# Four graph layers on one core: the opening's beta product in halves, scalings between relus, and a step order of its own for the second group

## The chip, the core and the metric

The kernel runs on one core of a Trainium2 chip. The metric is the device time of one execution in microseconds (us). Five engines work beside each other, each through its own list of instructions in order: the tensor engine (PE, for matmuls; its weight loads are counted apart as PEld), the vector engine (DVE), the scalar engine (ACT), GpSimd (POOL) and SyncE (SP). SP does nothing here but start DMA transfers, and POOL hardly more. An engine that waits for something holds back all that stands behind it in its list. Matmul results go to PSUM, which the kernel splits into two pools of four buffers.

## The reference

128 graphs of 64 nodes, with 512 features for each node, go through four layers, all in fp32. Each layer adds its result to x and normalizes the rows:

```python
# layer 0: hypergraph convolutions with H = (adj != 0), w = adj's first row
#   conv(x, W, b) = D^-1 H B^-1 H^T (x W^T) + b
h = relu(conv(x, W1, b1))                 # 512 -> 1024
h = layer_norm(h, gamma, beta)
x = norm(x + conv(h, W2, b2) + x)         # 1024 -> 512
# layer 1: scores from y = x w, s = y a
A = exp(leaky(tanh((s_i + s_j) / 8) * 8)) * adj
A = A / rowsum(A) * rowsum(adj)
x = norm(x + A x w)
# layer 2: three graph convolutions, relu after the first two
x = norm(x + adj (relu(adj (relu(adj (x gW1) + gb1) gW2) + gb2) gW3) + gb3)
# layer 3: eight heads of attention
p = 0.33 softmax(mask(q k^T / 8)) + 0.33 adj + 0.33 exp(-adj)
x = norm(x + (p v) W_out + b_out)
```

## The kernel before

**Tiles and groups.** Two graphs make one tile of 128 rows (a "pair" in the code), and four tiles make one group of 512 rows. There are 16 groups. A product with a graph's matrix consists of small matmuls of 64x64: `graph_T` (L435 to 453) does it and turns the result for the next product. These are the records named gt_l (layers 0 to 2) and gt_l0h (the 1024 hidden features of layer 0); a call for two tiles is 64 records.

**Products with weights.** From the second group on, every product of a 512x512 block is done in seven smaller products instead of eight (`multiply`, L503). Four sums of the left matrix (`sums`, L471, named s_...) and four differences of the weight (t1 to t4) stand in for blocks. Their order is B11, T1, T2, B21, T3, B22, T4 (L37). After B11, T1 and T2 the PSUM buffer is copied or added to a bias (`snap`; names u_...), and after B21, T3, B22 and T4 DVE or ACT adds the parts into the destination (L531 to 542). Since B11, T2, T3 and T4 go through one buffer (names a_...), each of them waits until the one before it has been read. The other two buffers are named b_... and c_.... One of the seven products is 8 matmuls of 256 columns.

**The weights.** A `Stream` brings weights in the order of their use through a ring of 20 tiles (`pump`, L340), each tile one DMA on SP. For the first use of a weight (q = 0) its four blocks come, DVE makes the four differences (`make`, L256; four subtractions), and POOL's queue writes them to DRAM (L277), from where later groups load them. Before, all weights that are loaded by then are made when the running product reaches its fourth part, B21 (L364), and a first use gives all its 8 ring tiles back after its last part. W2 is special: it has to be scaled by gamma, 16 times `act.mul` (L298, names w2s), and beta times W2 is needed as a row, bw_bc: 32 matmuls into bwps and an ACT copy (`beta_times`, L303).

**The first group** (`first_group`) can't wait for differences and uses plain products of 32 matmuls a tile (`rows_of`, names pp). `hidden(p, n)` is one tile's half of layer 0's first product with the relu; then come the statistics, the roots (`root`, on ACT), the reciprocal and the normalization of h (names rs_h, hb). `wa` builds, in two visits, the row w a for layer 1: a diagonal dg on DVE, one matmul wa_ps, a copy.

**The order.** Two strings at the end of the kernel (L1179 to 1188) write the order by hand. `start` is the opening, and each instruction made in it stays at its place on its engine (`in_turn`, and the wrapper at L132, which is the line that the profile gives for nearly everything up to about 130 us). Then come the steps of `order`: a. is the first half (layers 0 and 1) of group `step`, b. the second half (layers 2 and 3) of the group before, t. the tail (v, softmax, W_out) of the one before that. Each word runs a generator to its next `yield`; `stops` of a product says where it may yield. `rows` and `prep` build the matrices of the next but one group. Outside the opening a scheduler may move instructions by priority; `behind(key)` holds one back until the last addition of the named product has been issued. In step 1 there is no tail.

Of the kernel before, what the change touches and what calls it, by code (L numbers as in the profile page):

```python
# [14 lines left out]
P = 128  # L15
# [7 lines left out]
Q = 256  # L23
# [18 lines left out]
def kernel(  # L42
# [182 lines left out]
    class Weight:  # L225
# [62 lines left out]

        def scale(self):

            quads = []
            for u, raw in enumerate(self.raw):
                s = big.tile([P, 4, 2, Q], FP, name=f"{self.name}s_{u}", tag="big")
                b = {}
                for n, (k, m) in enumerate(((0, 0), (0, 1), (1, 1), (1, 0))):
                    for c in range(2):
                        f = (u * 2 + k) * 2 + c
                        act.mul(s[:, n, c], raw[:, n, c], ga_col[:, f : f + 1])  # L298
                    b[k, m] = s[:, n]
                quads.append(b)  # L300
            return quads

        def beta_times(self):  # L303

            bb = sp.tile([P, DH // P, P], FP, name="bb", tag="s")
            nc.gpsimd.tensor_copy(bb, be_col.unsqueeze(2).to_broadcast([P, DH // P, P]))
            ps = ps_gt.tile([P, 2, Q], FP, name="bwps", tag="gt")
            for n in range(2):
                for c in range(DH // P):
                    u, k, kc = c // 4, c // 2 % 2, c % 2  # L310
                    ten.matmul(
                        ps[:, n, :], bb[:, c, :], self.raw[u][:, ((0, 1), (3, 2))[k][n], kc, :],
                        start=(c == 0 and n == 0), stop=(c == DH // P - 1), skip_group_check=True,
                    )
            act.copy(bw_bc, ps.rearrange("p n f -> p (n f)"))

    w_1 = [Weight(W1T, n * D, f"w1{'ab'[n]}") for n in range(2)]
    w_2 = Weight(W2T, 0, "w2", halves=2, scaled=True)
# [7 lines left out]
    class Stream:  # L326


        def __init__(self, uses):
            self.todo = []  # L330
            for wt, q in uses:
                if q == 0:
                    self.todo.append((wt, q, None, 8))
                else:
                    self.todo += [(wt, q, what, wt.halves) for what in ORDER]
            self.here = {}
            self.held = 0
            self.to_make = []

        def pump(self):  # L340
            while self.todo and self.held + self.todo[0][3] <= RING:
                wt, q, what, n = self.todo.pop(0)
                self.held += n
                if q > 0:
                    self.here[wt, q, what] = [wt.load(q, what, u) for u in range(wt.halves)]
                elif wt in by_pairs:
                    by_pairs[wt] = None if wt.scaled else wt.load_quads()
                else:
                    self.to_make.append((wt, wt.load_quads()))

        def keep(self, wt):

# [8 lines left out]
        def take(self, wt, q, what):  # L361
            self.pump()

            if what == ORDER[3] or (q == 0 and (wt, q) not in self.here):  # L364
                for made, quads in self.to_make:
                    self.here[made, 0] = made.make(quads)
                self.to_make = []
            if q > 0:
                return self.here.pop((wt, q, what))
            return self.here[wt, q][what]  # L370

        def done(self, wt, q, what):

            if q > 0:
                self.held -= wt.halves
            elif what == ORDER[-1]:
                self.held -= 8
            self.pump()

    def load_wa():  # L380
# [122 lines left out]
    def multiply(lefts, wt_q, dst, key, flipped=False, res=None, stops=(3,)):  # L503


        acc = [ps_acc.tile([P, 2, Q], FP, name=f"{n}_{key}", tag="acc") for n in "ab"]

        def snap(ps, m, n, what):
            t = work.tile([P, 2, Q], FP, name=f"{what}_{key}", tag="w")
            if res is None:  # L510
                act.copy(t, ps)
            else:
                vec.tensor_add(t, ps, res(m, n))  # L513
            return t

        pa, pc = acc
        product(pa, lefts, wt_q, B11, True, False, flipped)
        s1 = snap(pa, 0, 0, "u1")
        if 1 in stops:
            yield  # L520
        product(pc, lefts, wt_q, T1, True, False, flipped)
        s5 = snap(pc, 1, 1, "u5")
        if 2 in stops:
            yield
        product(pa, lefts, wt_q, T2, False, False, flipped)
        s2 = snap(pa, 0, 1, "u2")
        if 3 in stops:
            yield
        pb = ps_acc.tile([P, 2, Q], FP, name=f"c_{key}", tag="acc")
        product(pb, lefts, wt_q, B21, True, True, flipped)  # L530
        vec.tensor_add(dst(0, 0), pb, s1)  # L531
        product(pa, lefts, wt_q, T3, False, False, flipped)
        vec.tensor_add(dst(1, 1), pa, s5)  # L533
        if 5 in stops:
            yield
        product(pc, lefts, wt_q, B22, False, True, flipped)
        last_add[key] = vec.tensor_add(dst(0, 1), pc, s2).ins  # L537
        product(pa, lefts, wt_q, T4, False, True, flipped)
        if res is None:
            act.copy(dst(1, 0), pa)  # L540
        else:
            vec.tensor_add(dst(1, 0), pa, res(1, 0))
# [112 lines left out]
    def first_half(g):  # L655
# [9 lines left out]
        for n in range(2):  # L665
            for i, _ in enumerate(multiply(
                [left], (w_1[n], q),
                lambda m, k: h[m][:, :, n * D + k * Q : n * D + (k + 1) * Q],
                f"l0w1{n}_{q}",
                res=lambda m, k: row2(b1_bc, n * D + k * Q),  # L670
                stops=(2, 3) if q == 1 and n == 0 else (3,),
            )):
                yield f"w1{'ab'[n]}{i + 1}"
            yield "w1" + "ab"[n]
# [77 lines left out]
        yield "c3"  # L752
        with behind(f"wo_{q - 2}"):
            left.sums()

        y = big.tile([P, G, D], FP, name=f"y_{q}", tag="big")
        for _ in multiply([left], (w_l1, q), nat(y), f"l1w_{q}", stops=(5,)):
# [21 lines left out]
    def first_group(g):  # L779
# [55 lines left out]
        for m in range(2):  # L835
            mv = small.tile([P, 2, 2], FP, name=f"mvh_0_{m}", tag="mvh")
            for p in range(2):
                hidden(2 * m + p, 1)
                if p > 0:
                    h_stats(2 * m, 1)  # L840
            h_stats(2 * m + 1, 1)
            for p in range(2):
                vec.bn_aggr(mv[:, p, :], sth[:, 2 * m + p].rearrange("p c s -> p (c s)"))
            rs = root(mv, f"h_0_{m}")
            vec.reciprocal(rs, rs)
            for p in range(2):
                normed(h[m][:, p, :], mv, rs, p)
        stream.used(w_1[1])
        yield "w1b"
        lefts = [Left(f"l0h{u}_0") for u in range(2)]  # L850
        for duo in range(2):
            for u in range(2):
                graph_T(
                    lambda p: h[p // 2][:, p % 2, u * D : (u + 1) * D], g["sm"], lefts[u].t, duo, f"l0h{u}_0"
                )
        yield "c2"
        hts = [left.t for left in lefts]
        s4 = small.tile([P, G], FP, name="s4_0", tag="s4")
        e = grp.tile([P, G, C], FP, name="e_0", tag="e", bufs=1)
# [92 lines left out]
        yield "c31"  # L952
        out_of_l1(2)
        out_of_l1(3)
        normed_l1(1)
        stream.used(w_l1)
        yield "l12"

    def second_half(g):
        q, xg = g["q"], g["x"]  # L960
# [62 lines left out]
                vec.tensor_add(xr, ps[p], xr)  # L1023
        yield "agg"

        with behind(f"wo_{q - 1}") if q < NGRP - 1 else nullcontext():
            layer_norm(xg, f"l2_{q}")
        left = Left(f"xT_{q}")

# [124 lines left out]
    def attend(g, duo, pts, v, left):  # L1154
# [22 lines left out]


    start = """  # L1179
        a0.c1 keep0 rest a0.w1a keep1 a0.w1b scale rows0 wa bw a0.c2 doubled0 constant0 rows1 a0.w20 keep2 wa prep1 a0.w21 a0.w22  # L1180
        a0.ss0 a1.c1 a0.w23 a0.den0 doubled1 a0.w24 a0.c30 a1.w1a1 a0.l10 a0.ss1 a0.l11 a0.den1 a1.w1a2 a0.c31 constant1 a1.w1a a0.l12
        a1.resid a1.w1b1 b0.gt a1.w1b keep3
    """.split()
    order = """
        t.v1 a.c1 t.v b.gt t.soft a.w1a1 a.w1a t.soft2 a.resid b.l2a1 b.l2a a.w1b1 t.ptp a.w1b t.pv a.lnh t.osum
        b.l2b1 a.c2a b.l2b a.c2b b.gb3 load a.w21 b.gh a.w2 rows b.l2c1 b.l2c2 a.ss b.l2c t.o1 a.den t.o2 a.c3 b.agg t.o
        a.p1 b.xT a.p2 b.q1 b.q t.ln3 b.k1 prep b.k b.dots
    """.split()
    lag = {"a": 0, "b": 1, "t": 2}
    todo = []  # L1190
# [7 lines left out]
            todo.append((what, 0, None))  # L1198
    n_start = len(todo)
    for step in range(1, NGRP + 2):  # L1200
        for what in order:
            who, dot, name = what.partition(".")
            key = (who, step - lag[who], name) if dot else (what, step + 1, None)
            if 0 <= key[1] < NGRP and key not in todo:
                todo.append(key)
# [17 lines left out]
    with in_turn(SP):  # L1223
        load_adn(first)
        w_2.load_raw()
    for n, (who, q, name) in enumerate(todo):
        opening[0] = n < n_start
        if who == "load":
# [2 lines left out]
        elif who == "rows":  # L1231
            if q > 0:
                preps[q] = prepare(groups[q])
            with behind(f"l0w2_{q - 1}") if q > 1 else nullcontext():
                next(preps[q])
        elif who == "prep":
            next(preps[q])
# [14 lines left out]
        elif who == "rest":  # L1252
            with in_turn(SP, POOL):
# [7 lines left out]
                gb2_col = load_col(gb2, KD, "gb2_col")  # L1261
                gb3_bc = load_row(gb3, D, "gb3_bc")
                bo_bc = load_row(bout, D, "bo_bc")
        elif who == "scale":
            by_pairs[w_2] = w_2.scale()
        elif who == "bw":
            w_2.beta_times()
        else:
            side = "a" if who == "a" else "b"
            if (side, q) not in gens:  # L1270
# [58 lines left out]
```

## Time and profile before

| | |
|---|---|
| median of 3 runs | 2818.47 us (2814.20 to 2824.47) |
| profiled execution | 2818.55 us |
| its span | 2816.8 us |
| PE busy | 2772.3 us |
| DVE busy | 2003.0 us |
| ACT busy | 819.1 us |
| POOL busy | 38.9 us |
| HBM traffic over the span | 143 GB/s |

The profile is one execution; its times count from the start of the span. Busy times of engines overlap. A row of the list of waits gives the engine and the operation that waited, the engine and the operation that released it, then the sum of the waiting time, the number of waits, and their mean. A row of the timeline gives the start, the length, the engine, the line, the operation with output<-input, and in brackets the idle time before it with what ended it; "issue" stands for a wait that the profile can't put down to another engine. The clock of PE is a share of the full clock, averaged over a stretch. A steady step, from the second on, takes 171.8 us; the opening and step 1 reach to about 390 us.

### The profile page before, as it was taken

What the parts mean: (1) busy time and instruction counts of PE and PEld (TensorE: products, weight loads), DVE (VectorE), ACT (ScalarE), POOL (GpSimd) and SP (SyncE); (2) the same over time, 40 slices, a digit from 0 to 9 for tenths busy, and PEclk for the clock granted to TensorE, in tenths of its full rate; (3) what the DMA queues carried; (4) which work ended last, traced back from release to release, by engine and by line L of the source; (5) the groups of instructions that cost most, each with busy time, mean ns of one, the idle gap of its engine ahead of it and who ended that gap; (6) DMA issues with size and microseconds to landing.
All of it is one profiled execution on the core that took longest, in us unless ns stands there. A gap on an engine that the chain in (4) does not pass through costs nothing.

```text
span 2816.8 us, 67748 instructions
## 1 busy us (share of the span) xinstructions
PE 2772.3 (98%) x28862; PEld 2365.4 (84%) x28862; DVE 2003.0 (71%) x3861; ACT 819.1 (29%) x1467; POOL 38.9 (1%) x72
## 2 busy tenths in 40 slices
PE   8999999999999999999999999999999999999998
PEld 7888888888888888888888888888888888888877
DVE  5677677676876767767677676767767677676756
ACT  3223323223232322323223223232323323232222
POOL 2010000000000000000000000000000000000000
PEclk9999999999999999999999999999999999999999
DMA  7354445454544545445454454545545454454441
GB/s 248 109 183 132 129 145 162 125 165 129 153 147 134 162 130 166 129 137 162 128 165 129 140 162 134 157 126 146 157 133 161 132 153 139 131 163 131 147 119 63
DMA packets 309661, 405.94 MB, mean 144 GB/s; under 512 B 57425, under 2 KB 184945, under 8 KB 309361
## 3 DMA queue, kind: packets, MB, share of 16 engines
q1 hardware_dynamic: 304384, 385.84, 46.3%
q0 software_dynamic: 4976, 15.76, 1.5%
q8 instruction: 229, 3.75, 0.6%
q14 instruction: 72, 0.58, 0.1%
HBM read 370.57 MB, written 30.93 MB: 143 GB/s over the span
## 4 chain that ended last, share of the span: by engine, by line
PE 85%; DVE 9%; issue 4%; ACT 1%; DMA 1%; POOL 0%; SPq 0%; DVEq 0%; POOLq 0%
PE a_l0w L496 13%; PE b_l0w L496 7%; PE a_l2b L496 4%; PE a_v L496 4%; PE a_k L496 4%; PE a_q L496 4%; PE c_l0w L496 4%; PE a_l2a L496 4%; PE a_l1w L496 4%; PE gt_l L445 3%; PE a_wo L496 3%; PE gt_l0h L445 2%; PE a_l2c L496 2%; PE b_l2b L496 2%; PE b_v L496 2%
## 5 line engine op out<-in xcount | busy, mean ns | idle before, releaser
L496 PE MATMUL a_l0w<-w2w,aT_l0h 128*128 128x256 f32 x720 | 164.3, 381 | 0.0
L427 DVE BATCH_NORM_STATS2 st_l<-x 128x6 f32<-128x512 f32 x248 | 160.3, 675 | 0.1
L496 PEld LDWEIGHTS a_l0w<-w2w,aT_l0h 128*128 128x128 f32 x720 | 135.6, 190 | 18.8
L681 ACT ACTIVATE h<-h 128x1024 f32<-128x1024 f32 x58 | 61.4, 1059 | 216.4 <-DVE h L537 194.9
L431 DVE TENSOR_SCALAR x<-x,mv_l,rs_l 128x512 f32<-128x512 f32 x248 | 120.1, 545 | 1.8
L453 ACT COPY aT_l<-gt_l 128x512 f32<-128x512 f32 x176 | 90.5, 601 | 72.8 <-PE gt_l L445 72.8
L496 PE MATMUL b_l0w<-w2w,s_l0h 128*128 128x256 f32 x480 | 108.5, 379 | 0.0
L496 PEld LDWEIGHTS b_l0w<-w2w,s_l0h 128*128 128x128 f32 x480 | 90.1, 190 | 13.5
L1002 ACT ACTIVATE aT_h<-gth,gb_col 128x256 f32<-128x256 f32 x128 | 48.5, 490 | 158.9 <-PE gth L994 158.9
L418 ACT ACTIVATE rs_l<-mv_l,eps_t 128x4 f32<-128x4 f32 (+1 forms) x63 | 18.9, 300 | 257.0 <-DVE mv_l L428 255.7
L496 PE MATMUL a_l2b<-gwbw,aT_h 128*128 128x256 f32 x360 | 86.9, 384 | 4.7 <-ACT aT_oT L1174 4.7
L496 PE MATMUL a_l2a<-aT_l,gwaw 128*128 128x256 f32 x360 | 86.6, 383 | 1.0 <-ACT aT_l L453 1.0
L496 PE MATMUL a_q<-aT_xT,wqw 128*128 128x256 f32 x360 | 86.6, 383 | 0.3 <-ACT aT_xT L1041 0.3
L496 PE MATMUL a_v<-wvw,aT_xT 128*128 128x256 f32 x360 | 86.7, 384 | 0.0
L496 PE MATMUL a_l2c<-gwcw,aT_h 128*128 128x256 f32 x360 | 85.3, 380 | 0.7 <-DVE g L533 0.7
L496 PE MATMUL a_wo<-wow,aT_oT 128*128 128x256 f32 x360 | 85.8, 381 | 0.1
L496 PE MATMUL a_l1w<-ww,aT_l 128*128 128x256 f32 x360 | 85.1, 379 | 0.0
L496 PE MATMUL a_k<-aT_xT,wkw 128*128 128x256 f32 x360 | 85.0, 379 | 0.0
L496 PE MATMUL a_l0w<-w1aw,aT_l 128*128 128x256 f32 x336 | 82.3, 388 | 0.0
L496 PE MATMUL a_l0w<-w1bw,aT_l 128*128 128x256 f32 x336 | 81.7, 379 | 0.0
L513 DVE TENSOR_TENSOR u_l0w<-a_l0w,b_bc 128x512 f32<-128x512 f32 x56 | 38.5, 688 | 59.8 <-PE a_l0w L496 59.8
L496 PEld LDWEIGHTS a_l2b<-gwbw,aT_h 128*128 128x128 f32 x360 | 67.1, 190 | 15.2 <-ACT aT_oT L1174 6.6
(503 smaller groups left out, 6474.0 us busy)
## 6 DMA issues: line engine op xcount, KB each, us to landing
w2w<-w2k SPq DMA_DIRECT2D x210, 256.0 KB, 2.7
x<-in_x_dram SPq DMA_DIRECT2D x15, 1024.0 KB, 6.2
w1aw<-w1ak SPq DMA_DIRECT2D x60, 256.0 KB, 2.7
w1bw<-w1bk SPq DMA_DIRECT2D x60, 256.0 KB, 2.7
ww<-wk SPq DMA_DIRECT2D x60, 256.0 KB, 2.7
gwaw<-gwak SPq DMA_DIRECT2D x60, 256.0 KB, 3.5
gwbw<-gwbk SPq DMA_DIRECT2D x60, 256.0 KB, 2.7
gwcw<-gwck SPq DMA_DIRECT2D x60, 256.0 KB, 2.7
```

The costliest lines, as they stand in the source:

```text
L418: act.activation(rs[:, at], mv[:, at, 1], AF.Sqrt, bias=eps_t)
L427: vec.bn_stats(st, xg[:, p, :])
L431: vec.tensor_scalar(xg[:, p, :], xg[:, p, :], mv[:, p, 0:1], rs[:, p : p + 1], ALU.subtract, ALU.mult)
L445: ten.matmul(ps[g][f * C : (f + 1) * C, c, p, :], src(2 * duo + p)[rows, c0 : c0 + C], mat[rows, 2 * duo + p, :], start=True, stop=True,)
L453: act.copy(o[:, :, :, g, :], ps[g])
L496: ten.matmul(acc[:, blk, :], lhsT, rhs, start=(first and blk == 0 and i == 0), stop=(last and i == n_k - 1), skip_group_check=True,)
L513: vec.tensor_add(t, ps, res(m, n))
L681: act.activation(hn, hn, AF.Relu)
L1002: act.activation(o[:, :, h, :], ps[h][:, c].rearrange("p (d a) i -> p d (a i)", d=2), AF.Relu, bias=gb2_col[:, k : k + 1],)
```

## The change

The change rearranges the opening and step 1. Matmuls, elementwise operations and transfers stay the same in kind and number.

1. `scale` becomes a generator with four parts: two blocks at a time (four `act.mul`) are done after each of the four `hidden(p, 1)` of the first group. Before, all sixteen followed the normalization of h.
2. `beta_times` takes its PSUM buffer from the pool of the weight products, `ps_acc`, and not from `ps_gt`. It yields between its halves: 16 matmuls stand ahead of each half of gt_l0h (`c20`, `c21`), and the copy follows the second half.
3. `Stream` makes a weight's differences at the B21 of the product just before that weight's first use, not of any weight that has come. In step 1, `sumsq` and `sumsk` make those of w_q and w_k earlier than that, at places in the order. A first use gives back its ring tiles part by part: two after B11, one after each other part.
4. The start order: `keep3` (the differences of layer 1's w) goes ahead of a1.resid, `a0.l12` ahead of a1.w1b1, and the last normalization of layer 1 for the first group becomes a part of its own, `l13`, behind a1.w1b1. The second stop of a1.w1a is after B21 instead of T2, and a1.w1b gets a stop after T1.
5. Step 1 has an order of its own, `step_1`: the third group's matrices (`rows`) stand behind b.k1 and are held until q's last addition; the layer norm of layer 2 for the first group is held until the sums of layer 1 for the second.

```diff
         def scale(self):
-            quads = []
+            self.quads = []
...
                         act.mul(s[:, n, c], raw[:, n, c], ga_col[:, f : f + 1])
                     b[k, m] = s[:, n]
-                quads.append(b)
-            return quads
+                    if n == 3:
+                        self.quads.append(b)
+                    if n % 2:
+                        yield
         def beta_times(self):
...
-            ps = ps_gt.tile([P, 2, Q], FP, name="bwps", tag="gt")
+            ps = ps_acc.tile([P, 2, Q], FP, name="bwps", tag="acc")
...
+                if n == 0:
+                    yield
             act.copy(bw_bc, ps.rearrange("p n f -> p (n f)"))
+            yield
...
-                    self.to_make.append((wt, wt.load_quads()))
+                    self.to_make[wt] = wt.load_quads()
+
+        def make(self, wt, q):
+            if q == 0 and wt in self.to_make:
+                with in_turn(DVE):
+                    self.here[wt, 0] = wt.make(self.to_make.pop(wt))
...
-            if what == ORDER[3] or (q == 0 and (wt, q) not in self.here):
-                for made, quads in self.to_make:
-                    self.here[made, 0] = made.make(quads)
-                self.to_make = []
+            at = self.uses.index((wt, q))
+            if what == ORDER[3] and at + 1 < len(self.uses):
+                self.make(*self.uses[at + 1])
+            if q == 0:
+                self.make(wt, q)
...
-            elif what == ORDER[-1]:
-                self.held -= 8
+            else:
+                self.held -= 2 if what == ORDER[0] else 1
...
         vec.tensor_add(dst(0, 0), pb, s1)
+        if 4 in stops:
+            yield
...
-                stops=(2, 3) if q == 1 and n == 0 else (3,),
+                stops=((2, 4), (2, 3))[n] if q == 1 else (3,),
...
+        last_add[f"l1s_{q}"] = next(
+            i for i in reversed(nc.cur_bb.bb.instructions) if i.engine == DVE
+        )
...
                 hidden(2 * m + p, 1)
+                next(scaling)
...
-        yield "c2"
+            yield f"c2{duo}"
...
-        normed_l1(1)
         stream.used(w_l1)
         yield "l12"
+        normed_l1(1)
+        yield "l13"
...
-        with behind(f"wo_{q - 1}") if q < NGRP - 1 else nullcontext():
+        with behind(f"wo_{q - 1}" if q > 0 else "l1s_1") if q < NGRP - 1 else nullcontext():
             layer_norm(xg, f"l2_{q}")
...
     start = """
-        a0.c1 keep0 rest a0.w1a keep1 a0.w1b scale rows0 wa bw a0.c2 doubled0 constant0 rows1 a0.w20 keep2 wa prep1 a0.w21 a0.w22
-        a0.ss0 a1.c1 a0.w23 a0.den0 doubled1 a0.w24 a0.c30 a1.w1a1 a0.l10 a0.ss1 a0.l11 a0.den1 a1.w1a2 a0.c31 constant1 a1.w1a a0.l12
-        a1.resid a1.w1b1 b0.gt a1.w1b keep3
+        a0.c1 keep0 rest a0.w1a keep1 a0.w1b rows0 bw0 a0.c20 wa bw0 a0.c21 doubled0 constant0 rows1 a0.w20 keep2 wa prep1
+        a0.w21 a0.w22 a0.ss0 a1.c1 a0.w23 a0.den0 doubled1 a0.w24 a0.c30 a1.w1a1 a0.l10 a0.ss1 a0.l11 a0.den1 a1.w1a2
+        a0.c31 constant1 a1.w1a keep3 a1.resid a0.l12 a1.w1b1 a0.l13 a1.w1b2 b0.gt a1.w1b
     """.split()
...
+    step_1 = """
+        b.l2a1 b.l2a a.lnh b.l2b1 a.c2a b.l2b a.c2b b.gb3 load a.w21 b.gh a.w2 b.l2c1 sumsq b.l2c2 a.ss b.l2c a.den b.agg
+        a.c3 a.p1 b.xT sumsk a.p2 b.q1 b.q b.k1 rows b.k prep b.dots
+    """.split()
...
-        for what in order:
+        for what in order if step > 1 else step_1:
...
-            with behind(f"l0w2_{q - 1}") if q > 1 else nullcontext():
+            with behind(f"l0w2_{q - 1}" if q > 2 else "q_0") if q > 1 else nullcontext():
                 next(preps[q])
```

More of the change, by code (lines that the diff above doesn't have):

```diff
@@ L337, in __init__ @@
             self.held = 0
-            self.to_make = []
+            self.to_make = {}
+            self.uses = uses
         def pump(self):
@@ L362, in take @@
             self.pump()
-            if what == ORDER[3] or (q == 0 and (wt, q) not in self.here):
-                for made, quads in self.to_make:
-                    self.here[made, 0] = made.make(quads)
-                self.to_make = []
+            at = self.uses.index((wt, q))
[3 more added lines that the diff above has]
+                self.make(wt, q)
             if q > 0:
@@ L848, in first_group @@
         stream.used(w_1[1])
+        by_pairs[w_2] = w_2.quads
         yield "w1b"
@@ L1225 @@
         w_2.load_raw()
+    scaling, bw_parts = w_2.scale(), w_2.beta_times()
     for n, (who, q, name) in enumerate(todo):
@@ L1263 @@
                 bo_bc = load_row(bout, D, "bo_bc")
-        elif who == "scale":
-            by_pairs[w_2] = w_2.scale()
+        elif who in ("sumsq", "sumsk"):
+            stream.make({"sumsq": w_q, "sumsk": w_k}[who], 0)
         elif who == "bw":
-            w_2.beta_times()
+            next(bw_parts)
         else:
```

## The prediction

> **What bounds the kernel now.** I read the page first, then busy time by stage, then the TensorE's (PE's) waits, then the timeline around the longest of them.
>
> ```profile
> span 2816.8 us, 67748 instructions
> ...
> PE 2772.3 (98%) x28862; PEld 2365.4 (84%) x28862; DVE 2003.0 (71%) x3861; ACT 819.1 (29%) x1467; POOL 38.9 (1%) x72
> ```
>
> PE is busy all but 44.5 us, so only that idle time, and PE work that runs slowly, can be won. By stage:
>
> ```profile
> 45.00:65.00 20.00, 15.99 (x304) 14.12 (x303) 14.18 (x40) 10.33 (x24) 3.71 (x6) 0.91 0.82 267
> 65.00:131.00 66.00, 61.53 (x579) 52.71 (x581) 46.37 (x93) 14.29 (x24) 4.34 (x8) 1.00 0.29 102
> 131.00:165.00 34.00, 31.73 (x341) 26.91 (x332) 22.53 (x42) 13.06 (x23) 6.50 (x12) 0.95 0.66 225
> 165.00:222.00 57.00, 52.39 (x601) 44.06 (x600) 41.74 (x88) 12.39 (x25) 5.42 (x10) 1.00 0.42 131
> 222.00:262.00 40.00, 39.93 (x286) 33.89 (x289) 29.85 (x58) 11.26 (x20) 3.45 (x6) 1.00 0.50 150
> ...
> 400.00:2680.00 2280.00, 2274.83 (x23734) 1942.43 (x23732) 1643.21 (x3149) 667.47 (x1194) 0.00 (x0) 1.00 0.49 145
> ```
>
> Columns: stretch, its length, busy us of PE, weight loads, DVE, ACT, POOL, then PE clock, DMA share, GB/s. The steady 2280 us hide 5.2 us of idle time, which this change does not reach. Between 45 and 222 lie 15.4 us in eight waits, and two stretches at a lower clock:
>
> ```profile
> PE gt_l L445 <- DVE t L747: 3.0, 1, 3.0
> PE a_l0w L132 <- DVE u_l0w L132: 2.9, 1, 2.9
> PE gt_l0h L132 <- issue: 2.5, 1, 2.5
> PE a_l2b L496 <- ACT aT_h L972: 2.3, 1, 2.3
> ...
> PE ss L728 <- DVE e L724: 1.6, 1, 1.6
> PE gt_l L132 <- DVE t L132: 1.6, 2, 1.1
> PE gt_l0h L132 <- ACT bw_bc L132: 1.5, 1, 1.5
> ```
>
> ```profile
> 44.17 6.50 ACT L132 ACTIVATE w2s<-w2r,ga_col 128x256 f32<-128x256 f32 x16
> 51.20 1.53 PE L132 MATMUL gt_l0h<-smat,h 64*64 64x64 f32 x86 [1.53 <-ACT bw_bc L132]
> 55.21 3.05 PE L132 MATMUL gt_l0h<-smat,h 64*64 64x64 f32 x104 [2.48 <-issue]
> 154.01 3.61 PE L496 MATMUL a_l2b<-gwbb,aT_h 128*128 128x256 f32 x8 [2.27 <-ACT aT_h L972]
> ```
>
> A burst of 128 gt records takes 2.02 us elsewhere; these 104 took 3.05 instead of 1.64. Eight 256-wide records take 1.73 us elsewhere, here 3.61. So each cold stretch (clock 0.5 for 3.41 us in the trace) cost about 1.7 us. All that could be won is 15.4 + 3.4 = 18.8 us.
>
> **The change, part by part.** Times are on the clock of before; what earlier parts won is left out until the sum. The orders are those in which the changed kernel's instructions are built. [...]
>
> *1. Beta in halves, scalings between relus (41 to 67 us).* Before, bwps (32 records, 7.07 us) sits in a buffer of the pool that gt_l0h needs, and the copy bw_bc that frees it stands behind 16 scalings (0.406 us each): 1.53 us. Then 256 gt records run in a row, and PE stops after 152 of them for "issue". The trace has a 16 KB packet of the instruction queue starting at 52.76, as PE stopped at 52.73. After, bwps is in the other pool, its halves (16 records, 3.45 us) stand before each burst of 128, so PE goes 41.41, 44.9, 46.9, 50.4, 52.4. The bw_bc wait is gone. Whether the fetch is late again is unknown: below by 0, above by the same 2.5 us + 1.4; I take 0 to 1.2, as PE now needs 5.5 us rather than 4.3 for the same number of instructions.
> The price is on ACT. Eight scalings and the 1.28 us table load now stand before the two roots: the first moves from 37.37 to 39.0 (four scalings), and the second, with four scalings behind each of the last two relus, from 43.97 to 46.25. DVE's reciprocal at 44.30 follows at 46.58: 2.28 later. DVE then runs without a pause to hb, so hb ends at 59.46 + 2.28 = 61.74. PE does its first product by 59.4, wa_ps by 59.8, and waits for dg (61.4) and hb; the 16 sps records (0.62) end at 62.5. Before, the next product began at 67.41: **4.9 won**. A late fetch of up to 1.6 us is hidden by this DVE wait.
> The six w2k stores on POOL's queue go out from about 35 instead of 45.36, beside w1bk's; their readers come after 139. Work that is hidden costs nothing here; uncovered, a store costs its 7.66 us landing.
>
> *2. Statistics and sums at other places (100 to 131).* c_l0w now stands ahead of gt_l, over the reciprocal: 1.10 of wait goes. But the order that DVE then has is h<-c_l0w (0.69), reciprocal (0.16), two normalizations (1.00), four constants (2.74), h<-a_l0w (0.69): from u_l0w's end at 107.25 these run to about 112.6. T4 of the product writes the buffer that the last of them reads, and could start at 111.8: 0.9 comes back. T4 starts at 112.7, not 113.17: 0.5. After it DVE does the four wt differences (2.4, formerly at 142.9) and four statistics (2.47) before the two products of l1 are added; u_l0w of B11 then ends at 123.9, PE needs it at 124.8. The 2.88 wait goes, with about 0.3 of restart. The normalization of pairs 2 and 3 (1.0) ends at 126.9, inside the first half of gt_l: **3.7 won** in all. Earlier wt tiles take ring places that gwab and gwbb had, so on SP these eight loads stand behind PE's products and two wk stores: gwbb may land by about 117.7 + 7.7 + 2.7 = 128; its first reader on DVE is at 143.5. Nothing.
>
> *3. 131 to 165.* DVE no longer has the wt differences, so h_0 is normalized at about 150.6 and PE fills the wait for the relus with 58 gt_l0h records (0.92 us). The relu that the first a_l2b needs ends at 153.8 rather than about 154.0: 1.2 of idle stays, 1.1 goes, and the cold 1.7: **2.7 won**.
> [...]
>
> *4. 196 to 235.* The third group's matrices (some 1.5 us of DVE between x and e) leave this stage; but g (0.6) is now ahead of e, so ss starts at 207.1 instead of 207.40. The four wqt differences (2.4) stand before t, so den comes no earlier. Then agg (2.31) runs over the 1.75 reciprocal, but its second half needs den's buffer: gt_l starts at 216.9, not 216.73, yet agg is behind it. a_l1w starts at about 219.1, not 221.06. The layer norm waits until after the sums; xtp still fits between products: a_q at 233.1 instead of 235.10: **2.0 won**.
>
> *5. 235 to 263.* wkt's four (2.4) are now ahead of qT<-a_q: T4 of q waits about 0.75. Behind q DVE does x (2.3), the matrices (3.95) and wvt (2.4), so kT<-a_k is late: T4 of k waits 0.6. rbps and sps stand after k, and dot waits for rb's copy, about 0.25. Against 0.7 of idle and inserted work before: **0.95 lost**. The adn and wb loads move five DMAs down SP's queue; next use is a step later.
>
> *6. 360 to 400.* wot's differences and b_wo change places; the 0.67 wait is filled with 1.3 us of b_wo, and c_wo is cut in two. Zero, between +0.5 and -0.5. Earlier releases of ring places hardly change SP's order: zero, same bounds.
>
> Sum: 4.9 + 3.7 + 2.7 + 2.0 - 0.95 = 12.35. The profiled execution took 2818.55 (span 2816.8, 1.75 around it), 0.08 from the median 2818.47 of three (2814.20 to 2824.47), so no correction: 2818.55 - 12.35 = **2806.2**.
>
> **The rivals.**
> *The fetch is late again, longer.* Packets of the instruction queue have 16 KB (229 of them, 3.75 MB, on the page); against PE's 57,724 matmul and load records that is one for some 250 of its instructions, an estimate, and two bursts of 128 matmuls with their loads still hold 512. [...] For it: DMA moves 267 GB/s in this stage. Against it: the half product between. 2.5 + 1.7 - 1.6 hidden = 2.6 lost: 2808.8.
> *DVE is the new bound.* Parts 2, 4 and 5 put makes in the way of T4 products. If each of the four places costs 1.2 more than I counted, 4.8 go: 2811.0. For it: DVE was busy 29.85 of 40 us there.
> *Slower.* SP is a queue: gwab now waits at its head for PE, with gwbb, fourteen w2w and gwcb behind it. If gwbb lands after 143.5, DVE stops at gwbt, and everything behind it, one for one. It decides beyond 143.5 + 12.35, and a landing at 165 would give 2828. Nothing shows it: my landing is 128.
>
> **How the numbers follow.** The sum: 0.62, its own range 2801 to 2811. Fetch: 0.20. DVE: 0.13. Slower: 0.05. Bounds of the unknown costs and the runs' spread of about 5 us either way give 2800 to 2814.5. About 0.3% (8.5 us) is what a measurement of this kernel can tell from no change; below 2810.0 lie nine tenths of the first case, over half of the second, a fourth of the third: 0.71 faster, 0.24 same, 0.05 slower.
>
> **What would show it.** Right: no PE wait for bw_bc or u_l0w; clock 1.00 in 45 to 65 and 131 to 165; PE waits for dg/hb about 1 to 1.6 us, for T4 of l0w, q and k each below 1.2; dots about 12 us earlier. Wrong: "issue" with a cold stretch in gt_l0h, gwbt waiting for a DMA, or steps of the steady part not 171.8 us long.

## The result, and the profile after

The changed kernel takes 2806.06 us (median of 6 runs, 2804.13 to 2806.97), against 2820.75 us for the kernel before (median of 6, 2814.20 to 2824.47): a ratio of 0.9949, 95% interval 0.9936 to 0.9962. The forecast was 2806.2 us. The profiled execution was the fastest of the six, 2804.13 us; its span is 2802.3 us.

The page's head and the busy time by stage, with the same columns as before (the clock is the first number behind POOL). The changed kernel runs ahead, so the same stretch holds somewhat later work than before:

```profile
span 2802.3 us, 67764 instructions
...
PE 2769.3 (99%) x28862; PEld 2362.0 (84%) x28862; DVE 2003.7 (72%) x3861; ACT 818.2 (29%) x1467; POOL 38.1 (1%) x72
```

```profile
45.00:65.00 20.00, 19.41 (x288) 16.17 (x281) 19.32 (x49) 5.87 (x13) 2.39 (x6) 1.00 0.71 225
65.00:131.00 66.00, 65.11 (x655) 56.34 (x654) 50.87 (x101) 16.27 (x27) 6.87 (x13) 1.00 0.45 154
131.00:165.00 34.00, 33.04 (x385) 28.20 (x385) 22.98 (x45) 13.14 (x23) 2.16 (x4) 1.00 0.48 156
165.00:222.00 57.00, 55.46 (x514) 45.19 (x514) 39.44 (x79) 15.46 (x30) 4.32 (x8) 1.00 0.37 117
...
400.00:2680.00 2280.00, 2273.91 (x23823) 1942.30 (x23822) 1640.16 (x3144) 666.85 (x1194) 0.00 (x0) 1.00 0.49 145
```

PE is now busy 19.4 of the 20 us from 45 to 65, with DVE busy 19.3 beside it. Both stretches that ran below full clock have it back. PE's waits up to 400 us show what is left:

```profile
PE dps L132 <- DVE ht L132: 3.4, 1, 3.4
PE rbps L132 <- DVE dg L132: 2.3, 2, 1.7
PE ss L743 <- DVE e L739: 1.3, 1, 1.3
PE a_l2b L509 <- ACT aT_h L993: 1.0, 1, 1.0
...
PE a_l2c L509 <- DVE g L548: 0.6, 1, 0.6
PE gt_l L132 <- DVE t L132: 0.5, 1, 0.5
PE a_l0w L132 <- DVE h L132: 0.4, 1, 0.4
...
PE gt_l L458 <- DVE x L1044: 0.2, 1, 0.2
```

The waits for bw_bc, issue and u_l0w are gone, that of 3.0 us for t has become one of 0.2 for agg's x, and those for dg (0.59 of the 2.3 is new) and h are new. The 3.4 us for ht and the other 1.7 for dg belong to the first 9 us and were there before.

An execution doesn't begin at one pace: the first 128 records of gt_l took 4.24 us before and 3.85 after. So I measure stages from one record of PE to the next, in us, with bwps as the first mark:

| from | to | before | after | won | forecast |
|---|---|---|---|---|---|
| span's start | bwps | 41.41 | 40.45 | 0.96 | 0 |
| bwps | second product with w2s | 26.00 | 21.08 | 4.92 | 4.9 |
| there | gt_l of layer 2 | 62.82 | 59.17 | 3.65 | 3.7 |
| there | c_l2b | 32.88 | 30.57 | 2.31 | 2.7 |
| there | a_q | 72.00 | 70.36 | 1.64 | 2.0 |
| there | a_v | 27.87 | 27.90 | -0.03 | -0.95 |
| there | a_l2a of the last group | 2420.20 | 2419.75 | 0.45 | 0 |
| there | span's end | 133.61 | 133.06 | 0.55 | 0 |

The sum is 14.45 us, the difference of the two spans. In a second profiled execution of the changed kernel the five stages from bwps to a_v took 21.07, 59.17, 30.56, 70.34 and 27.89 us. A second one of the kernel before took 25.01, 62.81, 33.02, 74.06 and 27.95, since other waits than in the first were followed by half clock (that for t, with 0.50 from 214.52 to 217.93 us, and not that for issue); so what the first and the fourth stage are said to win depends on the execution of before (3.93 and 3.70 by this one).

### The profile page after: what moved, and what is told of

It reads as the page before. It is cut to its first block, busy times and chain, and to the rows that moved or that the text cites. A ratio compares the mean times of both kernels' runs of the same rounds, so it can differ in the third digit from the quotient of the medians.

```text
span 2802.3 us, 67764 instructions
## 1 busy us (share of the span) xinstructions
PE 2769.3 (99%) x28862; PEld 2362.0 (84%) x28862; DVE 2003.7 (72%) x3861; ACT 818.2 (29%) x1467; POOL 38.1 (1%) x72
## 3 DMA queue, kind: packets, MB, share of 16 engines
q8 instruction: 229, 3.75, 0.5%
## 4 chain that ended last, share of the span: by engine, by line
PE 86%; DVE 8%; ACT 1%; issue 0%; DVEq 0%
PE a_l0w L509 13%; PE b_l0w L509 7%; PE a_l2b L509 4%; PE a_q L509 4%; PE a_k L509 4%; PE a_v L509 4%; PE c_l0w L509 4%; PE a_l2a L509 4%; PE a_l1w L509 4%; PE gt_l L458 3%; PE a_wo L509 3%; PE a_l2c L509 2%; PE gt_l0h L458 2%; PE b_l1w L509 2%; PE b_v L509 2%; PE b_l2b L509 2%
```

## The experiments

**1. One part undone at a time, beside the changed kernel itself.**

> The changed kernel once more, as the reference for the three others of this set. Theory (the waits were moved or removed by the new order, so they stay away in every execution): 2806 us within 2, no PE wait over 1.5 us before 2680 us, and the step from 131 to 165 us at full clock again. Rival (a part of the 14.4 us was luck of one execution's clock): a wait of before comes back, or a stretch at half clock appears between 20 and 2680 us, and the time is 1.7 us or more above 2806.

> The changed kernel with its first part alone undone: bwps in the other pool, whole, and all scalings behind the normalization of h. Theory (the parts add up): the wait for bw_bc and the late instructions come back, 4.9 us lost, 2811 us; up to 1.7 more if the wait cools PE. Rival (what PE loses there it would have waited for dg and hb anyway, and later waits take the rest): under 1.5 us lost, 2807.5 or less.

```diff
-        a0.w1b rows0 bw0 a0.c20 wa bw0 a0.c21
+        a0.w1b scale0 rows0 wa bw0 bw0 a0.c20 a0.c21
...
-            ps = ps_acc.tile([P, 2, Q], FP, name="bwps", tag="acc")
+            ps = ps_gt.tile([P, 2, Q], FP, name="bwps", tag="gt")
...
-                next(scaling)
```

> The changed kernel with its start order undone behind a0.w24: keep3 last, l12 and l13 together ahead of a1.resid, the old stops. Theory: the waits for u_l0w and t and most of that for the relu come back, 3.65 + 2.3 = 5.9 us lost, 2812 us. Rival (making the weights at the product before is what freed DVE, not the order of the opening): under 2 us lost, 2808 or less.

```diff
-        a0.c31 constant1 a1.w1a keep3 a1.resid a0.l12 a1.w1b1 a0.l13 a1.w1b2 b0.gt a1.w1b
+        a0.c31 constant1 a1.w1a a0.l12 a0.l13 a1.resid a1.w1b1 b0.gt a1.w1b keep3
...
-                stops=((2, 4), (2, 3))[n] if q == 1 else (3,),
+                stops=(2, 3) if q == 1 and n == 0 else (3,),
```

> The changed kernel with the second step in the old order: the third group's matrices in their old place, no early differences for q and k, the layer norm not held. Theory: 1.6 us lost between 196 and 235 us and nothing in the stage behind it, 2807.7 us. Rival (the crowd behind q costs what it saves, as my sum had it for half): within 0.5 us of the changed kernel, or faster.

```diff
-        for what in order if step > 1 else step_1:
+        for what in order:
...
-        with behind(f"wo_{q - 1}" if q > 0 else "l1s_1") if q < NGRP - 1 else nullcontext():
+        with behind(f"wo_{q - 1}") if q < NGRP - 1 else nullcontext():
...
-            with behind(f"l0w2_{q - 1}" if q > 2 else "q_0") if q > 1 else nullcontext():
+            with behind(f"l0w2_{q - 1}") if q > 1 else nullcontext():
```

Medians of 5 runs: 2804.57 us for the changed kernel, 2811.16 without the beta part, 2812.05 without the start order, 2807.62 without the step order; the kernel before took 2822.18 (9 runs) on that chip. The ratios to it are 0.9942 (0.993 to 0.9954), 0.9965 (0.9953 to 0.9978), 0.9965 (0.9952 to 0.9977) and 0.9952 (0.9939 to 0.9966). The second profile of the changed kernel has no PE wait above 1.3 us and no half clock between 20 and 2680 us. No later stage pays a part back: without the beta part, bwps to the second product takes 26.12 us, and the four stages behind it, up to a_v, what they take after, within 0.02. Without the step order a wait of 2.3 us for t is back, and its two stages take 71.17 and 28.11 us instead of 70.36 and 27.90, 1.02 more and not the 1.6 expected.

The medians fall further than the stages say: 6.59, 7.48 and 3.05 us above 2804.57, where the stages from bwps to a_v account for 5.04, 5.22 and 1.02. In the profiled executions the rest lies ahead of bwps, in the steady part and in the tail, where executions of one kernel differ too. So the times alone don't give the step order's worth, and that its 2807.7 was met is luck.

One reading fell. Without the start order, with keep3 late again, I expected most of the relu wait back. The waits of that kernel from 20 us on:

```profile
PE a_l0w L132 <- DVE u_l0w L132: 2.9, 1, 2.9
PE gt_l L132 <- DVE t L132: 1.6, 2, 1.1
...
PE a_l2b L509 <- ACT aT_h L993: 0.9, 1, 0.9
```

Those of u_l0w and t returned, that for aT_h did not. In the profiled execution the missing part was made up by slow records behind the 2.9 us, which I had not counted: the eight of a_l0w took 3.57 us there, against 1.99 behind the same wait in the first profile. That stage took 64.39 us, 5.22 more than after, against the 3.65 of part 2. So the expected 2812 us was met by luck.

**2. The weight stream, and the beta part taken to pieces.**

> The changed kernel with the weight stream as before: all loaded weights are made at B21, a first use gives its ring tiles back at its end, sumsq and sumsk do nothing. The wait for the relu at 144 us stayed short both without the start order and without the step order, so neither of them alone shortened it. Theory (where gwbt is made decides it): the wait grows from 0.96 by about 1.3 us, 2807.3 us, and by 1.7 more where it cools PE. Rival (each of the orders is enough for it): the wait stays below 1.1 us and the time within 0.7 us of 2805.9.

```diff
-            at = self.uses.index((wt, q))
-            if what == ORDER[3] and at + 1 < len(self.uses):
-                self.make(*self.uses[at + 1])
+            if what == ORDER[3] or (q == 0 and (wt, q) not in self.here):
+                for made, quads in self.to_make:
...
-                self.held -= 2 if what == ORDER[0] else 1
+            elif what == ORDER[-1]:
+                self.held -= 8
```

2806.04 us (5 runs), as fast as the changed kernel in its first set. The wait for aT_h fell to 0.59 us and one of 0.67 for u_l2a took its place; c_l2b came 0.87 us later. So the new stream brings no more than these 0.87 us by itself, and it isn't what alone shortened the relu wait either.

> The kernel before with one change: bwps takes its buffer from the pool of the weight products. Theory (PE stops after some 150 of 256 small matmuls in a row because instructions come late): the wait for bw_bc of 1.5 us goes, the one of 2.5 us for issue stays, 1.5 us won. Rival (the late fetch was a result of the first stop): both go, and PE then waits only for hb at 59.5 us; 4.0 us won, 5.7 with the cold stretch.

```diff
-            ps = ps_gt.tile([P, 2, Q], FP, name="bwps", tag="gt")
+            ps = ps_acc.tile([P, 2, Q], FP, name="bwps", tag="acc")
```

> The kernel before with bwps in the other pool, profiled once more, since its first profiled execution was over 4 us shorter than its twelve others. Theory (the instruction fetch at the 152nd of 256 small matmuls is late by a length that changes from execution to execution): PE stops at the 152nd record again, now for 2 to 4 us and with a stretch at half clock behind it, and the time is 2819 to 2822 us. Rival: the stop is as short as the first time (0.26 us) and the time differs for another cause.

Here 1.5 us were expected or 4.0, and there is nothing: 2820.64 us (13 runs) against 2820.01, ratio 1.0001 (0.9993 to 1.001). Two timelines of this same kernel, first the execution of 2813.94 us, then that of 2821.09:

```profile
51.16 0.33 PE L132 MATMUL gt_l0h<-smat,h 64*64 64x64 f32 x2 [1.15 <-ACT aT_l0h L132]
51.64 0.57 PE L132 MATMUL gt_l0h<-smat,h 64*64 64x64 f32 x22 [0.15 <-ACT aT_l0h L132]
52.47 1.75 PE L132 MATMUL gt_l0h<-smat,h 64*64 64x64 f32 x104 [0.26 <-issue]
```

```profile
51.27 0.32 PE L132 MATMUL gt_l0h<-smat,h 64*64 64x64 f32 x2 [1.15 <-ACT aT_l0h L132]
51.75 0.57 PE L132 MATMUL gt_l0h<-smat,h 64*64 64x64 f32 x22 [0.16 <-ACT aT_l0h L132]
55.48 3.05 PE L132 MATMUL gt_l0h<-smat,h 64*64 64x64 f32 x104 [3.16 <-issue]
```

The wait for bw_bc has only changed its name. The copy of bwps stood behind sixteen scalings on ACT, and so do the copies of aT_l0h; the second burst now waits for those (1.15 + 0.15 us instead of 1.5). And PE stops behind the same record as before, 128 + 2 + 22 = 152, once for 0.26 us and once for 3.16; the 104 records behind it took 1.75 and 3.05 us.

> The changed kernel with all sixteen scalings behind the normalization of h, as before, and the beta product in halves. Theory (halves alone are enough to end the issue wait, and what is bound by DVE's hb can start as early as before): the second burst of gt_l0h waits up to 2 us for ACT's copies behind the scalings, which end at 50.6 us, but hb is ready at 59.5 instead of 60.5; within 1.5 us of the changed kernel. Rival (the scalings are what counts): 3 us or more slower, with PE waiting for ACT and the issue wait back.

```diff
-        a0.w1b rows0 bw0 a0.c20 wa bw0 a0.c21
+        a0.w1b scale0 rows0 bw0 a0.c20 wa bw0 a0.c21
...
-                next(scaling)
```

> The changed kernel with the beta product whole, both halves ahead of all gt_l0h, and the scalings between the relus. Theory (256 small matmuls in a row run out of instructions): the issue wait of 2.5 us comes back in the second half of gt_l0h; 0.6 of it is covered by what PE waits for DVE now, so 1.9 us slower, 3.3 if PE cools. Rival (the fetch was late for another reason, such as the transfers of that moment): no issue wait, within 0.5 us of the changed kernel.

```diff
-        a0.w1b rows0 bw0 a0.c20 wa bw0 a0.c21
+        a0.w1b rows0 wa bw0 bw0 a0.c20 a0.c21
```

With all scalings behind h's normalization but the product in halves: 2806.82 us (5 runs), 21.30 us from bwps to the second product. That keeps 4.70 of the 4.92 us. With the scalings between the relus but the product whole: 2810.97 us, its five runs 2811.03, 2805.00, 2811.10, 2805.83 and 2810.97, and 27.33 us for the stage in the profiled one:

```profile
47.63 2.91 PE L132 MATMUL gt_l0h<-smat,h 64*64 64x64 f32 x152
54.61 3.06 PE L132 MATMUL gt_l0h<-smat,h 64*64 64x64 f32 x104 [4.07 <-issue]
```

The stop behind record 152 is back, longer than the 2.5 us expected, with the cold stretch (104 records in 3.06 us). Two of the five executions were as short as the changed kernel's, so by their times the stop was short or absent there. Cutting the run of 256 small matmuls, with bwps in the other pool, is what carries the beta part; halves in the old pool were not run. The changed kernel's timeline shows the cut:

```profile
40.45 3.62 PE L132 MATMUL bwps<-w2r,bb 128*128 128x256 f32 x16
44.00 2.09 PE L132 MATMUL gt_l0h<-smat,h 64*64 64x64 f32 x128
46.02 3.72 PE L132 MATMUL bwps<-w2r,bb 128*128 128x256 f32 x16
49.67 2.10 PE L132 MATMUL gt_l0h<-smat,h 64*64 64x64 f32 x128
51.70 7.17 PE L132 MATMUL pp<-w2s,aT_l0h 128*128 128x256 f32 x32
...
60.32 0.67 PE L132 MATMUL rbps<-dg,bones 128*128 128x256 f32 x2 [0.59 <-DVE dg L132]
```

**3. The relu wait, before once more, and one step further.**

> The changed kernel with both the start order and the weight stream undone; each of them undone alone left the wait for the relu at 144 us short. Theory (either of them alone brings h's normalization ahead of the relus, and with it 58 records of gt_l0h to fill the wait): with both gone the wait is 2.3 us again with no gt_l0h ahead of a_l2b, beside the 2.9 for u_l0w and the 1.1 for t; 2813.4 us, up to 1.7 more where it cools PE. Rival (the step order alone is enough): the wait stays at 1 us, 2812 us.

The edit is that of the start order and that of the stream together; the step order and the beta part are left. 2813.15 us (10 runs), ratio 0.9977 (0.9968 to 0.9987). PE's waits from 20 us on:

```profile
PE a_l0w L132 <- DVE u_l0w L132: 2.9, 1, 2.9
PE a_l2b L504 <- ACT aT_h L988: 2.3, 1, 2.3
...
```

The relu wait is back in full, and a_l2b has no gt_l0h ahead of it. So the start order or the stream alone is enough; the step order isn't. For the stage from c_l2b to a_q it is the other way round: 70.30 us here, so the step order alone brings all of the 1.64 us, of which 0.83 stay without it; what brings those was not separated. In the changed kernel the relu wait reads so, with the roots of h on ACT behind it, after and before:

```profile
142.15 1.14 PE L458 MATMUL gt_l0h<-smat,h 64*64 64x64 f32 x58
144.25 0.70 PE L509 MATMUL a_l2b<-gwbb,aT_h 128*128 128x256 f32 x2 [0.96 <-ACT aT_h L993]
```

```profile
138.48 0.48 ACT L431 ACTIVATE rs_h<-mvh,eps_t 128x2 f32<-128x2 f32 x2 [2.54 <-DVE mvh L708]
```

```profile
154.48 0.47 ACT L418 ACTIVATE rs_h<-mvh,eps_t 128x2 f32<-128x2 f32 x2
```

From the last product of l2a (140.33; 149.86 before) to a_l2b are 3.92 us, against 4.15 before: the relu isn't much earlier. Its wait is filled, since the roots of h now run ahead of the relus, where before they ran behind them.

> The kernel before, profiled once more. Theory [...]: the waits of 2.3 to 3.0 us are the same, but those that cool PE are others[...]; the stop at the 152nd record of gt_l0h is there with another length. Rival (certain waits cool PE, others never): half clock again behind gt_l0h and a_l2b only.

This kernel is written with the changed one's generators, but its instructions, 67748 as before, have before's order. It took 2818.72 us. The wait for issue was 3.03 us, behind record 152 again. This is the table by windows of that execution; the clock stands ahead of the last two numbers:

```profile
50.68:54.09 3.41, 1.52 (x86) 1.38 (x87) 3.41 (x6) 1.97 (x4) 0.29 (x1) 1.00 1.01 382
54.09:57.50 3.41, 2.27 (x107) 2.15 (x107) 3.30 (x9) 1.42 (x3) 0.00 (x0) 1.00 1.05 394
57.50:60.92 3.42, 3.42 (x18) 3.01 (x17) 1.30 (x5) 0.63 (x2) 0.00 (x0) 1.00 0.92 318
211.10:214.52 3.42, 1.25 (x6) 0.76 (x4) 3.42 (x5) 0.59 (x1) 1.44 (x3) 1.00 0.44 168
214.52:217.93 3.41, 2.57 (x96) 2.58 (x100) 0.78 (x2) 0.54 (x2) 0.54 (x1) 0.50 0.38 141
```

Behind the issue wait the clock was 0.50 in the first profile and 1.00 here, and the 104 records took 3.05 us there and 1.75 here. Behind the wait for t, 3.0 us both times, it was the other way round: full clock in the first profile, and here 0.50 from 214.52 to 217.93 us. The stage took 74.06 us instead of 72.00. So it isn't certain waits that cool PE, and others never.

> The changed kernel with DVE's work moved twice more: the second group's dg and hb ahead of the additions of b2 and of the constants, and constant1 from ahead of a1.w1a to behind a1.w1b2, where DVE has 2.5 us of idle time. Theory: the waits for dg (0.59 us) and h (0.40 us) go, nothing else moves, 1.0 us won against the changed kernel, 2804.9 us. Rival (DVE is late at the next place): PE then waits for the first x after gt_l0h or for T3 of w1b, and nothing is won.

```diff
-        a0.c21 doubled0 constant0 rows1 a0.w20
+        a0.c21 rows1 doubled0 constant0 a0.w20
...
-        a0.c31 constant1 a1.w1a keep3 a1.resid a0.l12 a1.w1b1 a0.l13 a1.w1b2 b0.gt a1.w1b
+        a0.c31 a1.w1a keep3 a1.resid a0.l12 a1.w1b1 a0.l13 a1.w1b2 constant1 b0.gt a1.w1b
```

All waits of PE between 20 and 300 us:

```profile
PE ss L743 <- DVE e L739: 1.3, 1, 1.3
PE a_l2b L509 <- ACT aT_h L993: 1.0, 1, 1.0
PE gt_l L132 <- DVE t L132: 0.5, 1, 0.5
PE gt_l L458 <- DVE x L1044: 0.2, 1, 0.2
```

Both waits are gone, and the two stages took 20.25 and 58.50 us instead of 21.08 and 59.17, 1.50 us less. The time is 2804.92 us (5 runs; 0.9947 of the kernel before, 0.9935 to 0.996). That beats the kernel before; from the changed kernel with its medians of 2806.06 and 2804.57 it can't be told apart. In the profiled execution the start took 0.70 us and the tail 0.71 more than in the changed kernel's, which takes back nearly all of the 1.50.

## Why the prediction was right, point by point

- **Part 1 (4.9; measured 4.92).** The account was right: PE ended up bound by DVE's chain from the second root to hb, on which DVE ran without a pause from 45.27 to 60.5 us. That came earlier on the clock than I had it (reciprocal at 45.27 instead of 46.58, product at 61.53 instead of 62.5), but 0.96 of this lay ahead of bwps and came from no part of the change (last section). What I could not decide, whether the stop for issue would come again, the runs answer: in none of the eight profiled executions with the product in halves. The cover for it is smaller than I had it, 0.59 us of wait for dg and not up to 1.6. Beside the halves, the scalings between the relus are worth 0.2 us, and the other pool alone nothing.
- **Part 2 (3.7; 3.65).** The wait of T4 of l0w is 0.40 us, and no wait for u_l0w is left.
- **Part 3 (2.7; 2.31).** Fill of 58 records, rest of 0.96 us and a full clock, as forecast; its two terms, 1.1 and 1.7, make 2.8 and not 2.7. The switches between products were not counted: the 128 records of gt_l0h ran in three pieces of 1.14, 0.32 and 1.26 us instead of 2.10 in one, which is 0.6 more. The reason given was part of the truth: the start order, to which keep3's earlier place belongs, is one of two sufficient causes; keep3 by itself was not tried.
- **The clock in parts 1 and 3.** I counted the two cold stretches from the rows of one execution. A wait of 2.26 us for the relu had clock 0.50 behind it in the second profile of before too, from 153.08 to 156.49 us, and with the other pool the eight records behind one of 2.26 us took 3.68 us. But the issue wait of 3.03 us in that second profile had 1.00 behind it. Taking the rows was right, but treating "cold behind this wait" as a property of the kernel was not.
- **Part 4 (2.0; 1.64).** Moved to before's clock by the 11.83 us won ahead of it, ss started at 207.09 (forecast 207.1) and a_l1w at 219.05 (219.1). The missing 0.36 came behind: half of it where xtp cuts into b_l1w in three pieces instead of two, half at the first two products of l1w (3.75 us to the third, against 3.56).
- **Part 5 (-0.95; -0.03).** The mis-sized term. I had T4 of q 0.75 and T4 of k 0.6 us late behind DVE's crowd. DVE had done wkt by 226.9, and qT<-a_q ended at 232.1, as PE ended b_q: T4 of q began 0.15 us late and T4 of k 0.03, too short for the list of waits. What made room is in DVE's order: two of wvt's four and the last normalization of layer 1 (1.9) stood ahead of qT<-a_q before, and behind it after. Of the costs forecast here only the 0.25 around dot shows in full (2.28 us to the next product, against 2.03). The terms written there make 0.90 and not 0.95.
- **Part 6 and the rest (0; 0.45 and 0.55).** b_wo came forward with six of its eight records, but the wait it was to fill kept 0.56 of its 0.67 us. The 0.45 is no more than two executions of the changed kernel differ by in that stage (0.52). Beside the last 0.55 stands the clock in the tail, 12.4 us at half speed before and 10.3 after; no run separates it.
- **Rivals.** The stop for issue would have come with the product whole (4.07 us there). DVE as the new bound: of the T4 of l0w, q and k only the first waited noticeably, 0.40 us. The slower case: DVE began gwbt at 133.97 and waited for no DMA.

That the forecast of 2806.2 met the time within 0.14 us is luck. It took 12.35 us off an execution of 2818.55, which then stood at the median; with six runs the median is 2820.75, and the gain is 14.69. Between the two profiles the five stages that the parts are about won 12.49 of the 14.45 us, and these were counted from one execution of before with two cold stretches, where others have other ones.

## What to carry to other kernels

Ahead of moving work, ask of each wait what else stands behind the same cause: another buffer for bwps won nothing, since the next copies stood behind the same scalings. 256 small matmuls in a row stopped PE for issue here, for 0.26 to 4.07 us, and with half of a product of 7.07 us ahead of each 128 of them no such stop was left. Compare stages between marks and not on the clock of the span: stages without half clock or a stop for issue repeat to 0.03 us here, where whole runs of a kernel differ by 3 to 10.

## What the runs showed of the hardware that I had not expected

- **The stop for issue.** Before (two executions), with the other pool (two) and with the whole product, PE stopped behind the 152nd of 256 small matmuls, for 2.48, 3.03, 0.26, 3.16 and 4.07 us; with the beta part undone it waited 2.7 us for issue in gt_l0h. In the first profile the third 16 KB packet of the instruction queue began at 52.76 us and took 0.94; PE stopped at 52.73 and went on at 55.21. In the changed kernel's profile the third packet began at 45.42 us and took 1.44, and the 153rd record started at 50.07 without a stop. That the stop is a wait for this packet is my reading of these times, in the expectations too; no run shows it by itself.
- **The half-clock stretches.** In the first profile's records of the clock they start at 55.24, 154.22, 2789.31 and 2813.21 us, in the changed kernel's at 2777.00 and 2797.48. The first two are 3.413 us long and 29 times that apart; the last two of before are 7 times, those of after 6 times that apart. In the 3.41 us ahead of the first three of before PE was idle for 2.48, 2.27 and 1.96 us, and ahead of the first of after for 2.61. The wait for t in the first profile, cut into stretches of 3.413 us counted from the same starts, lies in two, with 1.95 and 1.07 us of idle time, and the clock behind it was 1.00. These figures give no limit: 1.95 us stand ahead of full clock and 1.96 ahead of half. What they show is that one and the same wait goes both ways. Behind 2.87 us for u_l0w the eight records took 2.00 us with the other pool and 3.57 without the start order. The changed kernel has no wait above 1.3 us in its opening behind the first 9 us, and its 11 runs lie within 2.9 us, where the 6 of before's first sets span 10.3 and the 9 to 17 of its later sets 6.3 to 8.3.
- **The start.** The first 128 records of gt_l took 4.24 us before and 3.85 after, against 2.1 later, though the windows show the clock as full. The traces' own records of the clock begin at 14.28 us before and at 12.20 after, and PE's pace changes there. After, eight records of gt_l took 0.213 us up to 12.2 us and 0.117 behind it. Before, they took 0.213 to the end of gt_l, and the records of pp came 0.43 us apart at 13.7 us and 0.216 from 14.4 us on. An estimate from this: 2.08 us more at half pace would cost 1.04, and 0.96 were measured up to bwps. Two executions of before already differ by 0.51 there (41.41 and 40.90), so I don't put the 0.96 down to the change.
